# Norm factors, output order and filler steps of the soft-disc layer in a four-layer image kernel

## The chip, the cores and the metric

The kernel runs on one core of a Trainium2 chip. A core has five engines that work at the same time and wait for each other through semaphores: TensorE (PE, matrix products, with weight loads on a path of their own, PEld), VectorE (DVE), ScalarE (ACT), GpSimd (POOL) and SyncE (SP, which here only starts transfers). The metric is the device time of one execution in microseconds (us), as the median of several runs; lower is better.

## The reference

The input is eight images of 32 by 32 tokens with 256 channels in fp32. Four layers follow one another, each of the form x = x + layer(group_norm(x)). Only the last layer is changed:

```python
qkv = silu(x @ w_qkv.T);  q, k, v = split(qkv, 3)
q, k = rope(rms_norm(q, w_qn)), rope(rms_norm(k, w_kn))     # per head of 32
wp = silu(x @ w_wp.T + b_wp);  width_raw, sharp_raw = split(wp, 2)
width = sigmoid(width_raw) * max_dist + 0.5
sharp = sigmoid(sharp_raw) * 9.5 + 0.5
scores = einsum(q, k in a 7x7 window) * 32**-0.5
soft_mask = sigmoid((width - rel_dist) * sharp)
attn = softmax(scores - (1 - soft_mask) * 10000)
out = rms_norm(attn @ v_window, w_on)                        # over 256 channels
return silu((out + v) @ w_out.T)
```

(The rope turns q and k of one head by the same angle at every token, so it falls out of their product and the kernel has no step for it.)

## The kernel before, in words

Channels lie on the 128 partitions, so an image is two chunks of 128 channels (J = 2b + c, four heads each) by 1024 tokens. In `layer3` the attention of a chunk is cut into 8 groups of two 8 by 8 blocks of queries against a window of 14 by 14 keys; with 8 images that makes 128 groups n. A group goes through `DiscStream`:

- `scores(n)`: 8 small products of 32 channels on PE, into four PSUM banks;
- `soft(n)`: four ACT tanh, the disc mask, written into one of nine `e` tiles; `masked(n)`: POOL adds the window's edge;
- `logits(n)`: DVE joins scores and mask and takes the row's extreme;
- `exps(n)`: four ACT exponentials with their sums; `divide(n)`: DVE reciprocal, POOL product;
- `turn(n, 0 and 1)`: eight PE transposes, each four copied by DVE (`pts`); `values(n)`: 12 PE products, copied by DVE into `oT`.

The order on PE, ACT, DVE and POOL is written out by hand: the loop over n at the end of `layer3` emits, in step n, scores(n+3), exps(n), filler units due at n, logits(n+3), turn(n-2, 0), soft(n+5), divide(n), units due at n+0.5, turn(n-2, 1), values(n-3), masked(n+5). All PSUM tiles share one ring of 8 banks. Every engine takes its instructions in the emitted order.

All other work of the layer is a `Fillers` unit with a due step, so that it falls between the groups. For chunk J, n = 8J; for image b, n = 16b:

- `project(J, s, h)` (s = 0 q, 1 k, 2 v; h = half of 512 tokens): two PE products, ACT tanh, DVE product (silu), POOL square for q and k. k and q are due at n-12 to n-10.5, v at n-7.5 and n-7.
- `roots(J, t)`, due at step 8J-8: sums of squares on PE for the two halves of q and k (rows 0 to 127 of one bank) and, for the image two back, of the attention output; then ACT computes exp(-0.5 ln(.)). Ln needs another ACT table than tanh, so two table loads go with it.
- `head_scale(J, s, h)`: spreads one 32-row strip of the factors to 128 partitions by a PE product with K = 32 (`fac_ps`), and DVE multiplies q or k by it. Four units per chunk, due at n-6, n-5.5, n-5, n-4.5.
- `vturn(J, u)`: four PE transposes of the padded v, copied from PSUM by ACT (`v<-vt`). Five units per chunk.
- `tail_sq`, `tail_scale(J, b, c, h)`, `output(b, m, h)`, `reload(b, m, h)`: the end of an image: POOL squares, the norm's factor by a PE product with K = 32 whose weights `won` hold w_on, DVE product, POOL add of v, output projection, silu, residual add, store. tail_scale at n+30 to n+31.5, outputs at n+33.5, 39, 39.5 and 41.5.
- `gn.stats`, `gn.mean`, `gn.root`, `normed`, `discs(b, u)`: the next image's statistics, its normalised copy `xq` (ACT), and the gates of the discs: 16 PE products of 128 columns, then a chain DVE, ACT, DVE, ACT, DVE, DVE, DVE on 128 by 64 values.

A unit may return its second half; `units(at)` collects these in `later`, and `finish()` runs them, two times in a step:

```python
def finish():
    while later:
        later.pop(0)()
```

## Time and profile before

| what | value |
|---|---|
| runs | 3299.59, 3302.94, 3300.57 us; median 3300.57 |
| profiled execution | 3305.0 us, span 3303.2 us, so 1.8 us lie around the span |
| mean granted TensorE clock | 0.973 |
| layer 3, from its first group's exponentials to the end | 2531.9 to 3303.2 us of the span |
| head factors, L2144 | 128 PE instructions (64 products of two passes), 83.9 us busy |
| tail factors, L2177 | 64 PE instructions (32 products), 33.4 us busy |
| copies of the turned v on ACT, L1771 | 80, 573 ns each |
| tanh of the soft mask, L2103 | 512, 543 ns each |
| exponentials, L1715 | 512, 453 ns each |
| ACT table loads in layer 3 (L2136, L2103, L2027) | 18 + 16 + 2, 1283 ns each |

An fp32 product is two PE instructions, one per pass. "Busy" of a line is the union of its instructions' times, so products that run side by side in the array count once. The ends of matmuls are modelled; the distance from one start to the next is the safer figure. The profiled execution lies 4.4 us (0.13%) above the median.

### The profile page before, as it was taken

How to read it: one execution, taken by the hardware profiler on the slowest of the kernel's cores; microseconds unless marked ns; L12 is line 12 of the kernel's file. 1: busy time of each engine (PE TensorE's matmuls, PEld its weight loads, DVE VectorE, ACT ScalarE, POOL GpSimd, SP SyncE). 2: the span in 40 equal slices, each digit the busy share in tenths (PEclk: the TensorE clock that was granted, in tenths of full speed). 3: DMA queues.
4: the chain of work that ended last, by engine and by line, in shares of the span. 5: the costliest groups of instructions: out<-in, count | busy, mean ns of one | idle time of the engine just before them, and what ended most of it. 6: DMA issues, size and time to landing. Idle time of an engine off the chain costs nothing. (4 is left out here: it accounts for less than half of the span.)

```text
span 3303.2 us, 76346 instructions
## 1 busy us (share of the span) xinstructions
PE 3165.7 (96%) x30280; PEld 1638.2 (50%) x30280; DVE 2192.5 (66%) x5570; ACT 2278.5 (69%) x5066; POOL 1792.1 (54%) x1201
## 2 busy tenths in 40 slices
PE   7999999999998999899999999999998899999997
PEld 2323323323322444777777656666664555555554
DVE  4777777777785677565655546666664667777775
ACT  3667667667776567666555547677676878888885
POOL 4666666666663111344444445433436668788777
PEclk9999999999999999999999999999998879999999
DMA  3000000000011667787867630111111001110001
GB/s 142 1 26 10 17 26 1 26 26 1 26 39 57 235 233 260 208 206 204 182 192 205 182 138 28 66 41 40 53 55 44 2 14 40 34 37 30 27 27 62
DMA packets 139177, 267.92 MB, mean 81 GB/s; under 512 B 9218, under 2 KB 77700, under 8 KB 130500
## 3 DMA queue, kind: packets, MB, share of 16 engines
q1 hardware_dynamic: 132436, 242.67, 24.3%
q10 hardware_dynamic: 6384, 20.37, 1.8%
q8 instruction: 239, 3.92, 0.5%
q14 instruction: 118, 0.97, 0.1%
HBM read 177.81 MB, written 85.20 MB: 80 GB/s over the span
## 5 line engine op out<-in xcount | busy, mean ns | idle before, releaser
L694 DVE TENSOR_TENSOR e<-s,ret 128x1024 f32<-128x1024 f32 x512 | 602.1, 1217 | 174.4 <-PE s L688 171.9
L701 ACT ACTIVATE ea<-e 128x1024 f32<-128x1024 f32 x512 | 535.5, 1055 | 257.3 <-DVE e L694 234.9
L703 POOL TENSOR_TENSOR ea<-ea 128x1024 f32<-128x1024 f32 x128 | 304.1, 2376 | 284.9 <-ACT ea L701 216.9
L688 PE MATMUL s<-qk,qk 32*128 32x512 f32 x2048 | 302.1, 640 | 4.3 <-POOL qk L571 1.7
L1591 POOL TENSOR_TENSOR e<-e,su 128x616 f32<-128x616 f32 (+2 forms) x128 | 157.3, 1229 | 268.7 <-DVE su L1590 241.9
L740 PE MATMUL num<-e,v 128*32 128x512 f32 x2048 | 271.3, 595 | 0.0
L1738 DVE COPY pts<-pt 112x512 f32<-112x512 f32 x256 | 175.8, 687 | 137.5 <-PE pt L1733 135.7
L2103 ACT ACTIVATE e<-win,disc 128x196 f32<-128x196 f32 x512 | 239.5, 543 | 0.2
L1723 POOL TENSOR_TENSOR e<-e,su 128x784 f32<-128x784 f32 x128 | 191.4, 1495 | 87.9 <-DVE su L1722 62.0
L870 PE MATMUL up_ps<-x,wup 128*128 128x512 f32 x512 | 230.2, 604 | 4.0 <-POOL x L236 3.2
L1715 ACT ACTIVATE e<-e,mx 128x196 f32<-128x196 f32 x512 | 227.9, 453 | 0.0
L2110 POOL TENSOR_TENSOR e<-e,win 128x784 f32<-128x784 f32 x128 | 201.7, 1576 | 38.5 <-issue 31.6
L1282 POOL TENSOR_TENSOR decayed<-state,rb 128x520 f32<-128x520 f32 x48 | 50.8, 1058 | 304.2 <-PE sc L1215 112.7
L1586 ACT ACTIVATE e<-e,mx 128x154 f32<-128x154 f32 (+2 forms) x512 | 212.2, 425 | 0.0
L1086 ACT ACTIVATE d<-d,cols 128x128 f32<-128x128 f32 x512 | 163.9, 392 | 68.5 <-POOL d L1077 68.4
L713 PE MATMUL sm<-ea,ones 128*32 128x512 f32 x1536 | 208.8, 604 | 1.6 <-POOL ea L703 1.6
L897 DVE SCALAR_TENSOR_TENSOR cv<-xm,par,cv 128x512 f32<-128x512 f32 x192 | 144.7, 754 | 85.8 <-ACT cv L892 81.2
L2042 PE MATMUL qkv_ps<-xq,w 128*128 128x512 f32 x384 | 192.2, 627 | 1.2 <-ACT fac L2137 1.2
L1823 PE MATMUL qkv_ps<-x,w 128*128 128x512 f32 x384 | 182.7, 613 | 1.6 <-POOL x L236 1.6
L688 PEld LDWEIGHTS s<-qk,qk 32*128 32x128 f32 x2048 | 84.8, 182 | 197.2 <-issue 87.7
L1733 PEld LDWEIGHTS pt<-idg,e 128*112 128x112 f32 x1024 | 121.5, 140 | 122.5 <-issue 91.0
L1733 PE MATMUL pt<-idg,e 128*112 128x128 f32 x1024 | 166.5, 289 | 8.4 <-DVE oT L1757 3.1
(245 smaller groups left out, 6932.8 us busy)
## 6 DMA issues: line engine op xcount, KB each, us to landing
d<-l1rows SPq DMA_DIRECT2D x64, 512.0 KB
x<-x SPq DMA_DIRECT2D x25, 1024.0 KB
l1xm<-xm SPq DMA_DIRECT2D x16, 1024.0 KB
l1sz<-sz SPq DMA_DIRECT2D x16, 1024.0 KB
xv<-l1xm SPq DMA_DIRECT2D x32, 512.0 KB
l1xa<-xa SPq DMA_DIRECT2D x16, 1024.0 KB
xa<-l1xa SPq DMA_DIRECT2D x16, 1024.0 KB
rb<-l1rows SPq DMA_DIRECT2D x32, 512.0 KB
```

Source lines behind the costliest of these rows:

```text
L688: nc.tensor.matmul(s[:, j % 2], qk[b, 1, c][g, kb * P : (kb + 1) * P], qk[b, 0, c][g, h * HALF : (h + 1) * HALF], start=True, stop=True,)
L694: nc.vector.tensor_mul(e[n, i], s, m)
L701: nc.scalar.activation(ea[n, i], e[n, i], AF.Abs)
L703: nc.gpsimd.tensor_add(ea[n, i], ea[n, i], ea.pop((n - 1, i)))
L713: nc.tensor.matmul(acc["sm"][g, :], ones, two[j // 2][:, j % 2, :], start=kb == 0 and k == 0, stop=kb == 4 and k == 2,)
L740: nc.tensor.matmul(acc["num"][g, :], v[b][:, kb, vc], e[n, j // 2][:, j % 2, :], start=kb == 0, stop=kb == 7,)
L870: nc.tensor.matmul(ps, wup[:, kc, m * P : (m + 1) * P], seg(s)[:, kc], start=kc == 0, stop=kc == 1,)
L1586: self.nc.scalar.activation(p[:, j], p[:, j], AF.Exp, scale=-1.0, bias=mx[:, j : j + 1], accum_out=su[:, j : j + 1],)
L1715: self.nc.scalar.activation(e[:, j], e[:, j], AF.Exp, scale=-1.0, bias=mx[:, j : j + 1], accum_out=self.su[:, j : j + 1],)
L1733: self.nc.tensor.transpose(ps[: self.PART, at : at + P], self.tile(n)[:, 2 * i + j, k * self.PART : (k + 1) * self.PART], self.K.ident,)
L2103: nc.scalar.activation(e[:, j], win[:, 0], AF.Tanh, scale=disc[b][:, i, 8 + h : 9 + h], bias=disc[b][:, i, h : h + 1],)
L2110: nc.gpsimd.tensor_add(e, e, win[:, 1].unsqueeze(1).to_broadcast([P, 4, NWIN]))
```

## The change

The diff does seven things, all in layer 3 and its preparation. (1) `head_scale(J, s)` issues the products of both halves together, into two banks; there are two units per chunk, due at n-6 (k) and n-5 (q). (2) `tail_scale(J, b, h)` spreads the bare factor with a weight matrix that has ones in row 8 of each strip (`k_one8`), once for both chunks of channels; w_on is now a per-partition operand of the DVE product, which becomes a scalar_tensor_tensor. Two units per image instead of four, at n+27.5 and n+28.5. (3) `output` goes by half first, at n+29.5, 30.5, 31, 31.5, with reloads at n+26.5, 27.5, 28, 30.5. (4) The copy of the turned v goes from ACT to DVE, in the following `finish()`. (5) `discs` is due at n-13 and n-12.5 and its chain is cut into five parts, one per `finish()`; `finish()` keeps what a part returns for the next time. (6) In the steps with n a multiple of 8, `soft(n+5)` is emitted before the units, v's second half before `roots`, and a further `finish()` and `units(n + 0.25)` behind logits; `exps(n+1)` is emitted in step n in place of `exps(n)`. (7) The next image's statistics, its normalised copy and v's projections get other due steps.

```diff
@@ -88,6 +88,7 @@
         [(p[:, None] // 32 == np.arange(32)[None]) / 32.0, one / 256.0], 1
     ).astype(f)
     k["k_spread"] = (p[:, None] % 32 == p[None] // 32).astype(f)
+    k["k_one8"] = np.tile(p[:, None] % 32 == 8, (1, P)).astype(f)
     return {n: np.ascontiguousarray(v) for n, v in k.items()}
 
 
@@ -143,7 +144,7 @@
     a["l3_qkn"] = np.concatenate(
         [np.tile(i["L3_conv_w_" + n], 4) for n in ("qn", "kn")]
     )
-    a["l3_on"] = i["L3_conv_w_on"].reshape(2, P)
+    a["l3_on"] = _cols(i["L3_conv_w_on"])
     a.update(shape_constants())
     return {n: np.ascontiguousarray(v) for n, v in a.items()}
 
@@ -393,13 +394,11 @@
                 spread[:, 0], won[:, 0], -(32.0**-0.5) / MASK_SCALE, spread[:, 0],
                 ALU.mult, ALU.mult,
             )
-            nc.vector.memset(won, 0.0)
 
         def weight():
-            for h in range(2):
-                nc.sync.dma_start(
-                    self.won[32 * h + 8 : 32 * h + 9], a["l3_on"].unsqueeze(0)
-                )
+
+            nc.sync.dma_start(self.won[:, 0], a["k_one8"])
+            nc.sync.dma_start(self.won[:, 1, 0:2], a["l3_on"])
 
         return [loads, factors, weight]
 
@@ -1669,7 +1668,7 @@
 
     def __init__(self, K, wk, cp, pp, pairs, n_img, ebufs):
         super().__init__(K, wk, pp, pairs, n_img, ebufs)
-        self.slots, self.s = 20, {}
+        self.slots, self.s, self.su = 20, {}, {}
         shape = [P, 4, 2 * self.PART]
         self.tiles = [cp.tile(shape, F32, name=f"e{i}") for i in range(ebufs)]
 
@@ -1710,17 +1709,17 @@
 
     def exps(self, n):
         mx, e = self.mx.pop(n), self.prob(n)
-        self.su = self.wk.tile([P, 4], F32, name="su", bufs=4)
+        su = self.su[n] = self.wk.tile([P, 4], F32, name="su", bufs=4)
         for j in range(4):
             self.nc.scalar.activation(
                 e[:, j], e[:, j], AF.Exp, scale=-1.0, bias=mx[:, j : j + 1],
-                accum_out=self.su[:, j : j + 1],
+                accum_out=su[:, j : j + 1],
             )
 
     def divide(self, n):
-        e = self.prob(n)
-        self.nc.vector.reciprocal(self.su, self.su)
-        self.nc.gpsimd.tensor_mul(e, e, self.su.unsqueeze(2).to_broadcast([P, 4, NWIN]))
+        e, su = self.prob(n), self.su.pop(n)
+        self.nc.vector.reciprocal(su, su)
+        self.nc.gpsimd.tensor_mul(e, e, su.unsqueeze(2).to_broadcast([P, 4, NWIN]))
 
     def turn(self, n, i):
 
@@ -1768,7 +1767,7 @@
                 strips[:, col, 8 * r : 8 * r + 8].rearrange("p i j -> p (i j)"),
                 self.K.ident,
             )
-        self.nc.scalar.copy(
+        return lambda: self.nc.vector.tensor_copy(
             dst[: self.PART, 4 * u : 4 * u + 4, :],
             ps[: self.PART, :].rearrange("p (s c) -> p s c", c=P),
         )
@@ -1995,7 +1994,8 @@
         for i in range(3):
             st.clear(i)
         K.ring = st.ring
-        bwp, sel, spread, won = first.bwp, first.sel, first.spread, first.won
+        bwp, sel, spread = first.bwp, first.sel, first.spread
+        ones, on = first.won[:, 0], first.won[:, 1, 0:2]
         wo, win, eps = first.wo, first.win, first.eps
 
         gn = first.gn
@@ -2083,10 +2083,25 @@
                     d, ps.rearrange("p (t g) -> p t g", g=P)[:, :, 0:16],
                     bwp.unsqueeze(1).to_broadcast([P, 4, 16]),
                 )
-                th = wk.tile([P, 4, 16], F32, name="dth")
-                nc.scalar.activation(th, d, AF.Tanh)
+                return silu
+
+            def silu():
+                th = wk.tile([P, 4, 16], F32, name="dth", bufs=2)
+                nc.scalar.activation(th, disc[b][:, 4 * u : 4 * u + 4, :], AF.Tanh)
+                return lambda: silu2(th)
+
+            def silu2(th):
+                d = disc[b][:, 4 * u : 4 * u + 4, :]
                 nc.vector.scalar_tensor_tensor(d, th, 1.0, d, ALU.add, ALU.mult)
+                return sigmoid
+
+            def sigmoid():
+                d = disc[b][:, 4 * u : 4 * u + 4, :]
                 nc.scalar.activation(d, d, AF.Tanh, scale=0.5)
+                return scales
+
+            def scales():
+                d = disc[b][:, 4 * u : 4 * u + 4, :]
                 wd, sp = d[:, :, 0:8], d[:, :, 8:16]
                 md = math.sqrt(2.0) * 3
                 nc.vector.tensor_scalar(wd, wd, md / 2, md / 2 + 0.5, ALU.mult, ALU.add)
@@ -2138,14 +2153,17 @@
             nc.scalar.activation(r[:n], r[:n], AF.Exp, scale=-0.5)
             fac[J] = r
 
-        def head_scale(J, s, h):
-            g = slice(32 * (2 * s + h), 32 * (2 * s + h) + 32)
-            ps = st.ring("fac_ps")
-            nc.tensor.matmul(ps, spread[g, s], fac[J][g], start=True, stop=True)
+        def head_scale(J, s):
+
+            ps = [st.ring("fac_ps") for _ in range(2)]
+            for h in range(2):
+                g = slice(32 * (2 * s + h), 32 * (2 * s + h) + 32)
+                nc.tensor.matmul(ps[h], spread[g, s], fac[J][g], start=True, stop=True)
 
             def rest():
-                d = dest(J, s, h)
-                nc.vector.tensor_mul(d, d, part(ps))
+                for h in range(2):
+                    d = dest(J, s, h)
+                    nc.vector.tensor_mul(d, d, part(ps[h]))
 
             return rest
 
@@ -2164,22 +2182,26 @@
             b, c = divmod(J, 2)
             if u == 0:
                 st.v[b, c] = wk.tile([P, st.slots, P], F32, name="v", bufs=2)
-            st.value_unit(strips, st.v[b, c], u)
+            return st.value_unit(strips, st.v[b, c], u)
 
 
         def tail_sq(b, c):
             sqs["o", c] = wk.tile([P, L], F32, name="sq", bufs=4)
             nc.gpsimd.tensor_mul(sqs["o", c], st.o[b, c], st.o[b, c])
 
-        def tail_scale(J, b, c, h):
+        def tail_scale(J, b, h):
+
             g, hs = slice(32 * h, 32 * h + 32), slice(h * HALF, (h + 1) * HALF)
             ps = st.ring("fac_ps")
-            nc.tensor.matmul(ps, won[g, c], fac[J][g], start=True, stop=True)
+            nc.tensor.matmul(ps, ones[g], fac[J][g], start=True, stop=True)
 
             def rest():
-                d = st.o[b, c][:, hs]
-                nc.vector.tensor_mul(d, d, ps)
-                nc.gpsimd.tensor_add(d, d, vT[b, c][:, hs])
+                for c in range(2):
+                    d = st.o[b, c][:, hs]
+                    nc.vector.scalar_tensor_tensor(
+                        d, d, on[:, c : c + 1], ps, ALU.mult, ALU.mult
+                    )
+                    nc.gpsimd.tensor_add(d, d, vT[b, c][:, hs])
 
             return rest
 
@@ -2217,45 +2239,45 @@
             for i in range(4):
                 s, h = 1 - i // 2, i % 2
                 fill.add(n - 12 + i / 2, lambda s=s, h=h: project(J, s, h))
-                fill.add(n - 6 + i / 2, lambda s=s, h=h: head_scale(J, s, h))
-            fill.add(n - 7.5, lambda: project(J, 2, 0))
-            fill.add(n - 7, lambda: project(J, 2, 1))
+            for s in range(2):
+                fill.add(n - 5 - s, lambda s=s: head_scale(J, s))
+            fill.add(n - 8.5, lambda: project(J, 2, 0))
+            fill.add(n - 8, lambda: project(J, 2, 1))
             fill.add(n - 6, lambda: in_strips(J))
 
         def plan_image(b):
             n = 16 * b
             if b:
                 fill.add(n - 27.5, lambda: load(b))
+                ahead = (n - 23.75, n - 23.75, n - 22.5, n - 21.5)
                 for i in range(4):
                     fill.add(
-                        max(n - 23.5, -3) + i / 2,
+                        ahead[i] if b > 1 else -3 + i / 2,
                         lambda i=i: gn.stats(b, image_parts(x[b]), i),
                     )
                 fill.add(max(n - 21, -1), lambda: gn.mean(b, later))
                 fill.add(max(n - 19, 1), lambda: gn.root(b, later))
                 for c in range(2):
-                    fill.add(n - 13.5 + c / 2, lambda c=c: normed(b, c))
+                    fill.add(max(n - 15, 2) + c / 2, lambda c=c: normed(b, c))
                 for u in range(2):
-                    fill.add(n - 10 + u / 2, lambda u=u: discs(b, u))
+                    fill.add(max(n - 13, 4) + u / 2, lambda u=u: discs(b, u))
             for c in range(2):
                 fill.add(n + 19 + c, lambda c=c: tail_sq(b, c))
-                for h in range(2):
-                    fill.add(
-                        n + 30 + c + h / 2,
-                        lambda c=c, h=h: tail_scale(2 * b + 4, b, c, h),
-                    )
+                fill.add(n + 27.5 + c, lambda c=c: tail_scale(2 * b + 4, b, c))
+
+
             for i in range(4):
-                at = n + 32 + (1.5, 7, 7.5, 9.5)[i]
-                fill.add(at - 3, lambda i=i: reload(b, i // 2, i % 2))
-                fill.add(at, lambda i=i: output(b, i // 2, i % 2))
+                h, m = divmod(i, 2)
+                fill.add(n + (26.5, 27.5, 28, 30.5)[i], lambda h=h, m=m: reload(b, m, h))
+                fill.add(n + (29.5, 30.5, 31, 31.5)[i], lambda h=h, m=m: output(b, m, h))
 
         for J in range(2 * n_img + 3):
             b, c = divmod(J, 2)
             t = b - 2 if c == 0 and b >= 2 else None
+            if J < 2 * n_img:
+                plan_chunk(J)
             if J and (J < 2 * n_img or t is not None):
                 fill.add(8 * J - 8, lambda J=J, t=t: roots(J, t))
-            if J < 2 * n_img:
-                plan_chunk(J)
         for b in range(n_img):
             plan_image(b)
         for J in range(2 * n_img):
@@ -2272,18 +2294,20 @@
                     later.append(r)
 
         def finish():
-            while later:
-                later.pop(0)()
+
+            due = later[:]
+            later[:] = [r for r in [f() for f in due] if callable(r)]
+
+        def all_of(*rests):
+            while rests:
+                rests = [r for r in [f() for f in rests] if callable(r)]
 
         def start():
 
             units(-11)
             rest = [discs(0, 0), discs(0, 1), project(0, 1, 0)]
-            rest[0]()
-            rest[2]()
-            r = project(0, 1, 1)
-            rest[1]()
-            r()
+            all_of(rest[0], rest[2])
+            all_of(rest[1], project(0, 1, 1))
             soft(0)
             for h in range(2):
                 project(0, 0, h)()
@@ -2294,8 +2318,8 @@
             masked(0)
             roots(0, None)
             in_strips(0)
-            for i in range(4):
-                head_scale(0, 1 - i // 2, i % 2)()
+            for s in (1, 0):
+                head_scale(0, s)()
             masked(1)
             for i in range(3, 9):
                 st.clear(i)
@@ -2311,15 +2335,22 @@
                     if t is pairs[0]:
                         st.o[b, c] = wk.tile([P, L], F32, name="oT", bufs=5)
                     st.scores(n + 3)
-                if 0 <= n < N:
-                    st.exps(n)
+                if 0 <= n + 1 < N:
+                    st.exps(n + 1)
+
+                rooted = n % 8 == 0
+                if rooted and 1 < n + 5 < N:
+                    soft(n + 5)
                 units(n)
                 if 0 <= n + 3 < N:
                     st.logits(n + 3)
+                if rooted:
+                    finish()
+                    units(n + 0.25)
                 if 0 <= n - 2 < N:
                     st.turn(n - 2, 0)
                 finish()
-                if 1 < n + 5 < N:
+                if not rooted and 1 < n + 5 < N:
                     soft(n + 5)
                 if 0 <= n < N:
                     st.divide(n)
```

## The prediction

> **What bounds the kernel now.** I read the page first (busy shares, slices, clock), then the table of stretches cut at each image's first exponential in layer 3, then the chain of waits and PE's timeline there. Only layer 3's instructions change their order (before it, layer 2's end alone loses a memset of DVE and swaps two tiny loads), so everything up to 2487 us of the span stays.
>
> ```profile
> span 3303.2 us, 76346 instructions
> PE 3165.7 (96%) x30280; PEld 1638.2 (50%) x30280; DVE 2192.5 (66%) x5570; ACT 2278.5 (69%) x5066; POOL 1792.1 (54%) x1201
> PEclk9999999999999999999999999999998879999999
> ```
>
> The clock dips in slices 31 to 33, the start of layer 3. The stretches (us; busy time and instructions of PE, PEld, DVE, ACT, POOL; granted clock; DMA) are images 0, 1, 2, 3, then 6, 7 and the tail:
>
> ```profile
> 2531.90:2631.40 99.50, 91.72 (x849) 50.54 (x844) 61.43 (x254) 78.85 (x229) 60.95 (x46) 0.80 0.04 12
> 2631.40:2735.40 104.00, 98.32 (x906) 53.17 (x908) 64.52 (x252) 79.28 (x230) 66.02 (x49) 0.80 0.04 12
> 2735.40:2828.00 92.60, 90.08 (x964) 50.40 (x960) 69.44 (x268) 80.88 (x233) 73.97 (x56) 0.98 0.11 36
> 2828.00:2919.20 91.20, 88.69 (x972) 49.63 (x964) 69.36 (x268) 80.99 (x234) 74.06 (x56) 1.00 0.12 36
> ...
> 3101.50:3197.80 96.30, 94.00 (x960) 51.19 (x953) 66.26 (x257) 80.91 (x233) 73.35 (x55) 0.93 0.07 23
> 3197.80:3259.70 61.90, 55.41 (x755) 33.47 (x744) 45.40 (x190) 59.91 (x186) 52.01 (x37) 0.97 0.11 36
> 3259.70:3303.20 43.50, 32.04 (x206) 14.14 (x205) 17.01 (x36) 10.47 (x21) 27.25 (x21) 0.87 0.24 79
> ```
>
> A steady image takes 91.2 us; images 0, 1 and 6, with clock 0.80 and 0.93, take more though they have no more work. Is 88.7 us of busy PE real work? The chain of waits gives start-to-next-start costs (start, us, what):
>
> ```profile
> 2936.30 0.52 PE s L1692 x16
> 2936.83 1.05 PE fac_ps L2144 x2
> 2937.88 0.58 PE pt L1733 x4
> ...
> 2940.09 0.58 PE o L1749 x24
> ...
> 2943.54 1.72 PE qkv_ps L2042 x4
> ```
>
> By these rows and their neighbours (transposes 0.44 or 0.58, projections 1.72 or 1.92, vt 0.44, disc products 1.98, root sums 1.06 and 1.70) an image needs 16 x (0.52 + 0.58 + 2 x 0.51) = 33.9, 16 projections and outputs x 1.82 = 29.1, 12 factor products x 1.05 = 12.6, 10 vt = 4.4, discs 4.0, sums 3.8: 87.8 us. So PE waits only 3.4 us of 91.2 and sets the pace; ACT (80.9), POOL (74.0) and DVE (69.4) follow closely. The waits sit where the chain leaves PE: at the roots on ACT (two table loads of 1.28 us around 0.69 and 0.63, chain pieces from 2918.7 to 2926.9) and at the disc chain from 2955.3 to 2966.9.
>
> The half clock shows in two stretches, same columns:
>
> ```profile
> 2541.00:2558.10 17.10, 17.05 (x97) 7.81 (x98) 10.25 (x43) 14.70 (x44) 11.72 (x10) 0.50 0.20 61
> 2640.00:2663.90 23.90, 23.32 (x157) 11.15 (x158) 13.72 (x59) 15.35 (x48) 15.36 (x11) 0.50 0.14 45
> ```
>
> PE is busy throughout, at half speed. Each such stretch begins two or three steps after a chunk's v projection and ends within a window of the next full 128 by 128 projections (2557.59). In between only factors (32 rows), scores, transposes and values run.
>
> **The change part by part.** (1) *Paired head factors.* Two products in different 32-row strips. The trace has the case: in the start-up, four are adjacent. PE's timeline:
>
> ```profile
> 2512.17 1.14 PE L2144 MATMUL fac_ps<-fac,spread 32*128 32x512 f32 x8 [1.98 <-ACT fac L2138]
> ...
> 2748.60 1.12 PE L2144 MATMUL fac_ps<-fac,spread 32*128 32x512 f32 x2 [0.15 <-ACT v L1771]
> ```
>
> Four together (8 instructions) take what one takes alone, so a pair saves one unit: 1.05 us, about 2.0 at half clock (2542.67 to 2544.67). 15 chunks x 2 = 30 units. DVE's products stay. (2) *One tail factor for both channel chunks*: 2 units of 4 fall away per image, 16 in all. Together 46 x 1.05 = 48 us of PE at full clock, 6.3 per steady image: 87.8 to 81.5. DVE's product keeps form and size (0.68 us).
>
> The Trainium skill ("TensorE: Matmul & The Clock Gate", Part 3) gives 3.07x for four row tiles at N=512, where these rows give 4 x 1.12 / 1.14 = 3.9x. If a pair's loss is taken in proportion, my estimate from that page is 0.8 us saved per pair, 7 us less in all; the measured rows are used.
>
> (3) *v copies, ACT to DVE*: 10 per image x 0.57 = 5.7 off ACT (80.9 to 75.2); on DVE the same shape from PSUM is the pts copy, 0.69 us, so 69.4 + 6.9 = 76.3. Both stay below PE's 81.5, so it costs nothing in the sum; DVE is its cover, and in steps 1, 2, 6 (copies beside head products or vt) it is fuller than PE. If that cover fails PE waits for banks: up to 6.9 per image.
>
> (4) *Roots, soft first, exps one step ahead*: the same two loads per root (18 + 16 + 2 stay). Nothing is removed, but the mask that logits needs two steps later no longer queues behind 3.9 us of loads, Ln and Exp. Behind the root now stand exps(n+2), the second load, and soft of the next step; their users on DVE and PE come two to three steps later. (5) *Disc chain in five parts*: it no longer holds DVE and ACT while each waits for the other. (4) and (5) bear on the 3.4 us of waits: gain 0 to 3.4 per image; I take 0, because DVE and POOL get fuller. Statistics, norms and disc products in other steps: the same instructions and no DMA moved (the next image's load keeps its step); hidden as before under PE's pace, 0; if the norm (2 x 1.13 on ACT) now falls behind a root's loads with no slack, at most 2.3 per image.
>
> (6) *Outputs and reloads*: same four of each. On SP the last reload is one step ahead of its use instead of three; a reload takes about 3 us and a step 5.3, so it is covered; if not, POOL waits, at most 3 us per image, two steps of slack behind it. The three outputs of image 6 that now lie behind the loop move into it (3 x 1.8 of PE, in steps 121 to 127 where PE has idle time). For image 7 the order by half lets output projections start after two of four POOL adds (2 x 1.27 sooner), and no foreign tanh stands before the last root: tail -5, bounds 0 and -8.
>
> **Sum**, against the profiled 3305.0: images 2 to 5: 4 x 5.7 = 23 (6.3 less 0.6 for new waits). Images 0 and 1: four dipped chunks save two units of 2.0 each, 16, less 2 for dips that last longer: 14. Image 6 (one dipped chunk): 8. Image 7, where ACT sets the pace (59.9 of 61.9): 5 vt copies off ACT: 2. Tail 5. Together 52: 3253; the median lies 4.4 below the profiled execution: **3249**. Own range 3235 to 3262.
>
> **The rivals.** *Half gain.* Four engines now lie within 6 us of each other per image, and PSUM's 8 banks let PE lead DVE by about one step only. If DVE and POOL hold PE in the short steps, an image takes 88.5, images 0, 1, 6 gain half: 3274. For: in steps 1 and 2 PE needs 2.6 and 3.2 us by the rows above, while DVE's logits, copies, reciprocal and head products need about 3.3 and 3.9; and POOL meets strips, tail adds and squares in steps 10 to 13. Against: none of the sums passes 76.3.
>
> *Larger gain.* The waits go too (image 82.5, 4 x 8.7 = 35) and the half-clock stretches shorten, since discs now come in step 3 and bring full-array work: images 0 and 1 -13 each, 6 and 7 -14, tail -6: 3305 - 81 - 4.4 = 3219. For: most waits sit just where the order changes.
>
> *Slower: half clock in every chunk.* The change takes the second v projection (step 1) and one output (1.5) out of the stretch after the roots; in odd chunks steps 9, 10 and 11 then hold only small products. The clock falls although PE is busy: in the window 3114.5 to 3117.9 PE is busy 3.24 of 3.40 us and the next ones run at 0.50, with no more than factors, transposes, values and scores in it. A dip lasts 13.6 to 23.9 us and costs up to half, say 8. About six new ones eat the gain; in ten of the eleven chunks now free of a long one: 3249 + 80 = 3329. Against: the steady images have such steps (2 and 3, 10 and 11) already, with one short dip, and if PE is late it runs through them in 6 us.
>
> By the Trainium skill (same page, Part 1) the clock halves after an idle window of about 3.4 us and returns after a busy one. The rows disagree: it stayed at 0.50 for 17.1 us with PE busy for 17.05. By the page's rule a dip would cost some 1.7 us (an estimate) and this rival would never decide.
>
> *The change does nothing*: PE's unit is hidden by something else: 3301. The 3.4 us of waits speak against it.
>
> **How the numbers follow.** Forecast 0.45, half gain 0.25, larger gain 0.18, slower 0.09, nothing 0.03. Range 3208 to 3290: from beyond the larger gain to beyond half gain, leaving out the slower case, the null case and ends. The runs shown spread 3.3 us, so 0.2% (6.6 us) is what can be told from no change. Faster: 0.45 + 0.25 + 0.17 = 0.87; same 0.04; slower 0.09.
>
> **What would show it.** Right: pairs of factors as four instructions in about 1.14 us; the factor products of both lines busy some 60 us in layer 3 instead of 83.9 + 33.4; steady images near 85.5 with ACT 75, DVE 76; table loads still 36. Wrong: low clock in images 2 to 5 in steps 9 to 11; PE waits for pts, v or th in steps 1, 2 and 6; POOL waits for xr. The prediction fails if PE's busy share of a steady image falls below 90%, since then its saved units bought idle time.

## The result and the profile after

| kernel | median | runs | ratio to before | profiled execution | span |
|---|---|---|---|---|---|
| before | 3301.76 us | 3299.59 to 3305.27 (4) | 1 | 3305.0 us | 3303.2 us |
| after | 3253.18 us | 3249.47 to 3256.44 (4) | 0.9854 [0.9838, 0.9869] | 3252.73 us | 3250.8 us |

The time came out 4 us from the forecast of 3249. The terms behind it did not come out so well: two large ones missed, in opposite directions, so the closeness of the total is in part luck, and most of what follows is about that. The same page lines as before, of the changed kernel (span; busy time of each engine; granted clock by slice):

```profile
span 3250.8 us, 76370 instructions
PE 3117.7 (96%) x30248; PEld 1628.4 (50%) x30248; DVE 2244.0 (69%) x5649; ACT 2239.4 (69%) x4986; POOL 1799.2 (55%) x1201
PEclk9999999999998999999999999999999899999998
```

PE is 48.0 us less busy, ACT 39.1 less, DVE 51.5 more: the v copies have moved. The clock's dip where layer 3 begins (8, 8 and 7 in slices 31 to 33) has shrunk to a single 8, in slice 32.

To see where the 52.4 us of span went, layer 3 is cut at the same instructions in every kernel: VectorE's logits of group 3, 11, 19 and so on (line 1704 after), each eight steps later; the last cut is at group 127. Two such stretches are an image, the first called even, the second odd. "Low" is the time at half clock, from the clock records of the same trace. All in us.

| stretch | before | low | after | low | gained | forecast |
|---|---|---|---|---|---|---|
| images 0 and 1 | 205.6 | 81.6 | 173.9 | 17.1 | 31.7 | 14 |
| images 2 to 5 | 366.1 | 3.4 | 364.8 | 34.1 | 1.3 | 23 |
| image 6 | 96.4 | 13.7 | 85.4 | 0 | 11.0 | 8 |
| image 7, to group 127 | 56.3 | 3.4 | 47.1 | 3.7 | 9.2 | 2 |
| the rest | 47.8 | 11.2 | 46.5 | 19.2 | 1.3 | 5 |

(Layer 3 began 2 us later in the changed kernel's execution.) The four images that the forecast called steady gained next to nothing, and the first two twice what was expected. Here are an even and an odd stretch of the kernel before (us; busy time and instructions of PE, PEld, DVE, ACT, POOL; granted clock; DMA):

```profile
2829.30:2876.20 46.90, 44.44 (x492) 26.16 (x488) 34.34 (x135) 41.69 (x119) 37.96 (x29) 1.00 0.13 40
2876.20:2920.40 44.20, 44.15 (x472) 23.41 (x468) 34.91 (x135) 39.20 (x115) 36.00 (x29) 1.00 0.10 33
```

and the like in the changed kernel, an even and an odd stretch of a steady image, then the odd one of image 6:

```profile
2801.20:2841.20 40.00, 38.47 (x477) 24.01 (x476) 35.46 (x136) 37.59 (x112) 35.94 (x26) 1.00 0.15 48
2841.20:2891.20 50.00, 49.48 (x478) 26.40 (x477) 39.97 (x143) 38.59 (x112) 39.16 (x31) 0.93 0.09 28
...
3111.80:3157.20 45.40, 45.23 (x473) 24.37 (x472) 36.24 (x133) 38.35 (x112) 38.31 (x30) 1.00 0.10 33
```

The even stretch fell from 46.9 to 40.0; the odd one rose from 44.2 to 50.0, with a granted clock of 0.93 in place of 1.00. Image 6, with no half clock, took 85.4 (it has no statistics of a next image to compute; these are small on PE).

**What the pairs did.** PE's timeline in the changed kernel (start, us, what, idle before and its releaser): first a pair in image 0, then the two pairs of an odd stretch and what comes after them.

```profile
2538.48 1.13 PE L2161 MATMUL fac_ps<-fac,spread 32*128 32x512 f32 x4
...
2849.38 1.93 PE L2161 MATMUL fac_ps<-fac,spread 32*128 32x512 f32 x4
2851.24 1.08 PE L1732 MATMUL pt<-idg,e 128*112 128x128 f32 x8
2852.25 0.65 PE L1748 MATMUL o<-pts,v 112*32 112x128 f32 x24
2852.83 0.59 PE L1691 MATMUL s<-kp,qT 32*64 32x196 f32 x16
2853.37 1.72 PE L2161 MATMUL fac_ps<-fac,spread 32*128 32x512 f32 x4
```

The pair of image 0 takes what the prediction gave it, 1.13 us for four instructions. The other two take 1.93 and 1.72. From the start of the second to PE's next product pass 2.06 us, nearly as much as two single factors; 0.34 us of that PE is idle, because the next product (line 201) waits for a copy on DVE. The weight loads of that second pair (same columns) and VectorE's products with the pair before it tell why:

```profile
2853.37 0.29 PEld L2161 LDWEIGHTS fac_ps<-fac,spread 32*128 32x128 f32 x2 [0.30 <-DVE kp L2166]
2853.96 0.29 PEld L2161 LDWEIGHTS fac_ps<-fac,spread 32*128 32x128 f32 x2 [0.30 <-DVE kp L2166]
```

```profile
2852.64 1.27 DVE L2166 TENSOR_TENSOR kp<-kp,fac_ps 128x512 f32<-128x512 f32 x2
```

DVE multiplies by the first pair only at 2852.64, over three us after its first product, and is done at 2853.9. The second half of the next pair waits until DVE has finished (2853.91 against a weight load at 2853.96), so it starts 0.59 us after the first half instead of beside it. What PE needs from DVE there can only be a free PSUM bank; the factors were ready long before. Over the whole run this is the largest share of these weight loads' waits, 8.8 us (29 times):

```profile
L2161 PEld LDWEIGHTS fac_ps<-fac,spread 32*128 32x128 f32 x128 | 17.4, 182 | 20.3 <-DVE kp L2166 8.8 <-issue 3.9 <-DVE pts L1737 3.9
```

(the last columns: idle time of the weight queue before these loads, and what ended it). The four pairs of a steady image take 1.36, 1.65, 1.86 and 2.06 us from start to next start, 6.9 together, where eight singles took 8.4.

**What the clock did.** Three windows right after the second pair, same columns as the stretches above:

```profile
2852.40:2855.80 3.40, 3.06 (x47) 1.50 (x41) 3.37 (x10) 3.40 (x12) 3.34 (x4) 1.00 0.01 2
2855.80:2862.60 6.80, 6.80 (x52) 3.46 (x52) 6.20 (x24) 4.16 (x16) 4.54 (x5) 0.50 0.01 4
2862.60:2866.00 3.40, 3.40 (x12) 1.52 (x10) 2.10 (x10) 1.83 (x5) 2.78 (x3) 1.00 0.00 0
```

In the first window PE is busy 3.06 of 3.40 us, but with scores, factors of 32 rows and transposes. The next 6.8 us are granted half clock (0.50), though PE is busy throughout. The clock is back after the first projection of 128 by 128 (2861.71). The prediction's slower rival described this. In images 2 to 5 it happens in steps 11 to 13 of the odd stretches, 3.4 or 6.8 us each time, 23.9 us in all. The other 10.2 of the 34.1 us lie in even stretches and begin otherwise, behind waits of PE for DVE's qT (line 2052) of 1.86 and 2.61 us.

### The profile page after: what moved, and what is told of

The parts are those of the page before. It is cut to its first block, busy times and chain, and to the rows that moved or that the text cites. A ratio compares the mean times of both kernels' runs of the same rounds, so it can differ in the third digit from the quotient of the medians.

```text
span 3250.8 us, 76370 instructions
## 1 busy us (share of the span) xinstructions
PE 3117.7 (96%) x30248; PEld 1628.4 (50%) x30248; DVE 2244.0 (69%) x5649; ACT 2239.4 (69%) x4986; POOL 1799.2 (55%) x1201
## 5 line engine op out<-in xcount | busy, mean ns | idle before, releaser
L1704 DVE CUSTOM_DVE_ANT_0 e<-s,e 128x196 f32<-128x196 f32 x512 | 153.5, 354 | 12.8 <-POOL e L2125 11.3
L1732 PE MATMUL pt<-idg,e 128*112 128x128 f32 x1024 | 157.3, 284 | 4.8 <-POOL e L1722 2.2
```

## Experiments

All are timed with the kernel before beside them on the same chip, whose medians there were 3301.9, 3303.0, 3307.1 and 3307.2 us; so ratios are compared. The question behind them is whether the forecast's mechanism (PE units saved) holds and half clock takes part of it, or whether another part of the change (order, copies, discs, outputs) earned the time; a theory's letter counts for its run alone. The columns "even" and "odd" are the averages of images 2 to 5; all columns from "images 0, 1" on are of the profiled execution.

| kernel | median us | ratio [95%] | images 0, 1 | images 2 to 5 | low there | even | odd |
|---|---|---|---|---|---|---|---|
| before | 3301.8 | 1 | 205.6 | 366.1 | 3.4 | 46.9 | 44.6 |
| after | 3253.2 | 0.9854 [0.9838, 0.9869] | 173.9 | 364.8 | 34.1 | 41.6 | 49.6 |
| u1_single | 3260.3 | 0.9876 [0.9852, 0.9900] | 183.9 | 357.9 | 6.8 | 42.1 | 47.4 |
| h1_pairs_late | 3265.9 | 0.9892 [0.9865, 0.9919] | 181.7 | 369.2 | 37.5 | 42.3 | 50.0 |
| h2_v_mid | 3310.6 | 1.0025 [1.0013, 1.0037] | 187.9 | 395.7 | 54.6 | 51.1 | 47.8 |
| u6_order | 3321.6 | 1.0059 [1.0040, 1.0079] | 190.6 | 399.0 | 68.3 | 46.9 | 52.9 |
| h5_dummy | 3249.9 | 0.9841 [0.9824, 0.9859] | 177.4 | 359.2 | 10.2 | 41.3 | 48.5 |
| h4_disc_split | 3240.4 | 0.9811 [0.9797, 0.9826] | 170.7 | 355.0 | 3.4 | 39.4 | 49.3 |
| u5_disc_back | 3260.4 | 0.9870 [0.9855, 0.9884] | 177.1 | 368.4 | 30.7 | 40.6 | 51.5 |
| u4_v_act | 3269.0 | 0.9894 [0.9877, 0.9910] | 175.0 | 374.1 | 44.4 | 44.0 | 49.5 |
| h6_split_late | 3241.0 | 0.9809 [0.9782, 0.9836] | 169.7 | 355.7 | 13.7 | 39.8 | 49.1 |
| h7_split_single | 3237.7 | 0.9803 [0.9769, 0.9837] | 170.5 | 347.2 | 0 | 38.4 | 48.4 |
| b6_order | 3302.9 | 0.9999 [0.9980, 1.0018] | 198.8 | 377.8 | 30.7 | 48.6 | 45.8 |
| u3_outs_back | 3281.2 | 0.9937 [0.9914, 0.9960] | 170.0 | 379.9 | 41.0 | 51.8 | 43.2 |

**The pairing undone.** Four single factors per chunk, at their old dues (`head_scale` and the start-up, not shown, go back with the plan):

```
-            for s in range(2):
-                fill.add(n - 5 - s, lambda s=s: head_scale(J, s))
+            for i in range(4):
+                s, h = 1 - i // 2, i % 2
+                fill.add(n - 6 + i / 2, lambda s=s, h=h: head_scale(J, s, h))
```

> The change with the pairing of the head factors undone: four single units per chunk at n-6 to n-4.5, the rest as changed. A single unit takes 1.05 us from start to next start; the changed kernel's 30 pairs took 1.06 to 2.21, some 1.67 each. Theory A (pairs are half hidden: the second product waits for a PSUM bank): 30 x (2.10 - 1.67) = 13 us more, 3266. Theory B (the pairing is worth the full unit, as forecast): 31 to 40 us more, 3284 to 3293. Theory C (PE does not set the pace, the units are hidden): 3253.

7 us slower than the change, by medians; the intervals overlap. The parts point both ways: images 0 and 1 lost 10 us, with 20 more at half clock, and images 2 to 5 gained 7 although PE had more factors to do, since their half clock shrank from 34.1 to 6.8.

**The pairs half a step later**, after the products that hold their banks (`n - 5 - s` becomes `n - 4.5 - s`):

> The changed kernel with both pairs half a step later (n-5.5 and n-4.5), behind logits, the first transposes and a finish of the same step, when DVE has emptied four score banks. Theory A (the second product of a pair waits for DVE to free a bank): the four instructions start together, a pair takes about 1.07 us, some 18 us of PE time less; 3240 if PE sets the pace. Rival (two products alone do not run side by side in the array unless four are adjacent): pairs stay at 1.4 to 2.1 us and the time at 3253.

A miss in the time. The pairs did become cheaper (1.38, 1.06, 1.56 and 0.96 to 2.01 us from start to next start, 42.1 over the layer in place of 51.5), and the kernel no faster: 13 us slower by medians, though the intervals touch, with 8 us lost in images 0 and 1 and 4 in images 2 to 5, half clock in every odd stretch (6.8 us) and more often in the even ones.

**One full-width product more in odd stretches**, two accumulating 128 by 128 matmuls into a bank nobody reads (the unit `warm` itself is not shown):

```
+            if b:
+                fill.add(16 * b - 5, lambda b=b: warm(b))
```

> The changed kernel plus one full 128 x 128 product (K 256, 512 columns, 1.72 us on PE at full clock) at step 11 of every odd chunk but the last, into a bank that nothing reads: pure extra work. Theory D (the odd chunks of 49.4 us are long because a window with only small products halves the clock at step 11 or 12): low clock there vanishes, odd chunks 44.8 + 1.7 = 46.5, five dipped chunks gain 2.9 each, the undipped one loses 1.7: 3253 - 13 = 3240. Rival (low clock is a by-product of a wait): seven times 1.7 is added, 3265.

The odd stretches' half clock vanished, and 1.8 us of added work per image made the kernel no slower: 3249.9. The direction is shown; the size (3 us, not told apart from nothing by the intervals) is less than expected. The odd stretch fell only from 50.0 to 48.5.

**The second disc unit in that place instead**, work that must be done anyway:

```
-                    fill.add(max(n - 13, 4) + u / 2, lambda u=u: discs(b, u))
+                    fill.add((max(n - 13, 4), n - 5)[u], lambda u=u: discs(b, u))
```

> The changed kernel with the second disc unit (16 products of 128 columns at full array, 1.98 us) moved from step 3.5 of the even chunk to step 11 (n-5) of the odd chunk; nothing added. Theory D: low clock at steps 11 to 13 vanishes, odd chunks 44.8 + 2.0 = 46.8, even chunks 40.6 - 1.5 = 39 if one disc unit is enough for their clock: an image 86 instead of 90 to 92, five of them: 3253 - 23 = 3230. Rival (the even chunks then lose their own full-array work and dip): even 43 to 45, 3250.

3240.4 us: faster than before and than the change (the intervals do not overlap), though 10 us short of what was expected. Half clock in images 2 to 5 is back to 3.4 us. An image without any still takes 88.7 us (same columns as the stretches above):

```profile
2884.60:2923.90 39.30, 37.18 (x461) 22.40 (x460) 35.10 (x131) 37.30 (x110) 34.64 (x26) 1.00 0.17 49
2923.90:2973.30 49.40, 48.85 (x494) 26.89 (x493) 42.55 (x149) 39.03 (x114) 39.25 (x31) 1.00 0.09 29
```

PE is busy 86.0 of it, and half clock explains nothing here. So the pairs' price had to be tested without it, in the two runs told last.

**The v projection and the strips later**, to spread full-width work over the odd stretches:

```
-            fill.add(n - 8, lambda: project(J, 2, 1))
-            fill.add(n - 6, lambda: in_strips(J))
+            fill.add(n - 5.5, lambda: project(J, 2, 1))
+            fill.add(n - 4.5, lambda: in_strips(J))
```

> The changed kernel with the second half of v's projection moved from step 0 (n-8) to the middle of step 2 (n-5.5) of each chunk, and the strips from n-6 to n-4.5. Nothing is added. Theory D (in odd chunks the clock is halved because steps 9 to 12 hold only small products): full 128 x 128 work there keeps the clock at 1.00 in images 1 to 5, odd chunks fall from 49.4 to about 45 us, 3253 - 20 = 3233. Rival (the low clock only follows a wait and costs nothing itself): odd chunks stay near 49 us, 3253. Rival (later strips and v hold up the transposes of v): slower, 3260.

Slower than the kernel before. It kept the odd stretches at 47.8, and opened a wait of 7.9 us in the even ones. PE's timeline (idle time and releaser in brackets) and ScalarE's there:

```profile
2929.92 1.13 PE L2161 MATMUL fac_ps<-fac,spread 32*128 32x512 f32 x4
2938.98 3.51 PE L2075 MATMUL wp_ps<-w,xq 128*128 128x128 f32 x16 [7.93 <-DVE vT L2054]
```

```profile
2929.74 1.28 ACT L2118 ACT_TABLE_LOAD   x1
2931.03 1.88 ACT L2118 ACTIVATE e<-win,disc 128x196 f32<-128x196 f32 x4
2932.82 1.23 ACT L418 ACTIVATE xq<-x,gn 128x1024 f32<-128x1024 f32 x1
...
2935.71 1.86 ACT L2118 ACTIVATE e<-win,disc 128x196 f32<-128x196 f32 x4
2937.47 0.57 ACT L2027 ACTIVATE th<-qkv_ps 128x512 f32<-128x512 f32 x1
```

The tanh of the v projection (line 2027) stands on ACT behind a table load, two soft discs, a norm and four exponentials; DVE's product for vT waits for it, and a bank with it, and PE for the bank. After it the disc products run at half clock (3.51 us for 16; the next 16 take 1.95).

**The order inside a step undone** (exponentials, soft and finish where they were; nothing else):

> The changed kernel with the loop's order as before: exps(n) in step n, soft(n+5) behind the first finish in every step, no extra finish in root steps; the rest as changed. Theory E (the new order takes the waits at the roots off the chain): even chunks go from 40.6 back to 43 or 44 us, 16 x 2 to 3 us, 3285 to 3300. Rival (the order is worth nothing, the gain is PE's work and the outputs' place): 3253.

3321.6, slower than the kernel before: worse than both theories expected. In this kernel the order is worth 68 us. PE's longest waits in layer 3 say where part of it goes (us, times, longest):

```profile
PE fac_ps L2161 <- DVE pts L1737: 20.2, 14, 2.3
```

The second half of a pair now stands some 2 us for a bank, and half clock comes with it: such a wait of 2.06 us ends at 2830.15, and from 2830.3 on the clock is at half for 10.2 us. **The same order alone in the kernel before**:

> The kernel before with one part of the change only: the order inside a step (row exponents one step ahead, soft and finish moved round the roots). Undoing this order in the changed kernel cost 68 us, with 68 us at half clock in images 2 to 5. Theory N (the order matters there because the changed kernel has less PE work to cover waits behind ACT; the kernel before has 3.4 us at half clock in images 2 to 5 and gaps of only 2.5 us per image): gain of 0 to 25 us, 3278 to 3302, most of it in images 0 and 1 (205.6 us, of it 82 at half clock). Rival O (the order is worth the same anywhere): 3235 us, faster than the whole change.

Nothing: 0.9999 [0.9980, 1.0018]. Images 0 and 1 gained 6.8, image 6 gained 6.0 and images 2 to 5 lost 11.7. So the order is no gain that adds to the others. The kernel before has single factors, so the wait that the order spares the pairs of the changed kernel does not exist there; that this is the whole reason was not tried.

**The v copies back on ACT**:

```
-        return lambda: self.nc.vector.tensor_copy(
+        self.nc.scalar.copy(
```

> The changed kernel with the copy of the turned v back on ACT, at once behind its transposes. By the sums ACT would need 80.9 and DVE 69.4 of the 85 to 90 us of an image, so by the forecast's working the edit is worth nothing: 3253. Rival (ACT is late behind the roots' loads, the copy of step 1.5 queues there and holds its bank): one stall of 2 to 4 us per chunk, 3253 + 16 x 3 = 3300.

16 us slower by medians, where the prediction's sum had nothing: the copies' move earned time, in images 2 to 5 (9 us), image 6 (5) and the end (6). Half clock in images 2 to 5 rose by 10 us. The wait that the rival named is there:

```profile
PE s L1691 <- ACT v L1770: 13.9, 7, 2.2
```

Six of these seven waits last 2.20 us, and in five of the six cases half clock begins within 1.3 us of the wait's end, before or after it.

**The discs and norms back** to their old dues:

> The changed kernel with the disc units and the normalised copy at their steps of before (n-10, n-9.5; n-13.5, n-13), the chain still cut into five. Theory F (images 0 and 1 gained 32 us because the discs in step 3 or 4 bring full-array work early and keep or restore the clock): low clock returns in even chunks, 6 to 13 us each, even chunks 40.6 to 45, 3253 + 8 x 4 = 3285. Rival (the gain there is the loop's order alone): 3253.

7 us slower by medians, not 32, and the intervals overlap. Images 0 and 1 kept nearly all that they had gained; their half clock came back to 30.7 us, from 17.1, where the kernel before has 81.6. So the early discs freed them of a small part of it at most.

**Outputs, reloads and tail factors back** to their old dues (their order by halves kept):

```
-                fill.add(n + 27.5 + c, lambda c=c: tail_scale(2 * b + 4, b, c))
+                fill.add(n + 30 + c, lambda c=c: tail_scale(2 * b + 4, b, c))
...
-                fill.add(n + (29.5, 30.5, 31, 31.5)[i], lambda h=h, m=m: output(b, m, h))
+                fill.add(n + (33.5, 39, 39.5, 41.5)[i], lambda h=h, m=m: output(b, m, h))
```

> The changed kernel with the tail factors, reloads and output units at the dues of the kernel before (2.5 to 10 steps later; the order of their halves as in the changed kernel). In the trace the sixteen output products that took 7.05 us of PE in image 7 before are in images 0 and 1 in the changed kernel, and image 7 went from 56.3 to 47.1 us. Theory P (that move is what image 7 gained, and only moves work about): image 7 back to 54 to 56, images 0 and 1 shorter by 5 to 7 or the same if PE waits there instead, the tail 48; 3253 to 3262 us. Rival Q (the units also give PE full-width work that keeps the clock up in images 0 and 1): images 0 and 1 go from 174 back to 190 us with 20 us or more at half clock, 3275 us or more.

28 us slower, and neither theory foresaw where: image 7 went to 53.6, the end to 49.5 and images 0 and 1 to 170.0, near P, but images 2 to 5 lost 15 and image 6 lost 7. PE's waits over layer 3 (us, times, longest) and the timeline show it:

```profile
PE fac_ps L2161 <- DVE th L2219: 13.6, 11, 2.3
```

```profile
2803.10 1.12 PE L2161 MATMUL fac_ps<-fac,spread 32*128 32x512 f32 x2
2806.54 1.12 PE L2161 MATMUL fac_ps<-fac,spread 32*128 32x512 f32 x2 [2.32 <-DVE th L2219]
```

An output product runs one step ahead of the pair (2799.31); its bank is free only when DVE has done the output's last product (line 2219). The second half of the pair needs a bank and stands 2.3 us. This is the pairs' weakness again, with another holder. Five of these waits last 2.32 us, and half clock begins within 2 us of the end of each, before or after it.

**Pairs cheap and the clock up, both at once**: the second disc unit at `n - 5` and the pairs half a step later.

> The changed kernel with two moves together: the second disc unit at due n - 5 instead of n - 12.5 (step 11 of each odd chunk, as in h4_disc_split, which took 3240.4 us), and the paired head factors half a step later (as in h1_pairs_late, where a steady image's pairs take 42.1 / 8 = 5.3 us of PE against 6.9 in h4_disc_split, but half clock came to steps 11 to 13). Theory K (two separate deductions from the forecast: pairs that wait for a PSUM bank, and half clock in odd chunks; each move mends one): 88.6 - 1.6 = 87.0 us per image in images 2 to 5, no half clock there, 3240 - 7 * 1.6 = 3229 us. Rival L (later pairs take PE's cover out of steps 11 to 13 again, disc unit or not): half clock of 6.8 us in odd chunks, 3250 us or more.

The pairs took 39.6 us over the layer in place of 51.6 in h4_disc_split, a 12 us saving of PE, and the time did not move (3241.0 against 3240.4). K fell; L too, since the 13.7 us of half clock in images 2 to 5 all lie in the even stretches. **Split discs with single factors**:

> The second disc unit at due n - 5 and the pairing undone (four single head factors per chunk at their old dues): what the pairing is worth once half clock is out of the comparison. Theory K: in h4_disc_split the eight pairs of an image take 6.9 us of PE and the sixteen single factors of the kernel before 8.4, so singles cost 1.5 us per image, 12 in all: 3252 us (the prediction's step 1 would say 4.2 per image and 3274). Rival M: single factors free their banks in turn, so the waits of the logits and turns near the pairs vanish too and nothing is lost: 3240 us or less.

3237.7, no slower than with pairs: h6_split_late, beside it on the same chip, has 3241.0, and the intervals overlap. M holds: a loss of a few us would not show in these intervals, but the 34 us of the prediction's step 1 would. (An image has four pairs, or eight singles; the "eight" and "sixteen" of the expectation are twice that, its us are right.) Of all kernels tried this has the lowest median, and its ratio and those of the two others with split discs lie below the change's. Where PE's time in layer 3 goes, summed from each product's start to the next start (waits and half clock included; totals of the profiled executions, of which h7's, 3231.9 us, lies 5.8 below its median):

| product | before | after | h4_disc_split | h6_split_late | h7_split_single |
|---|---|---|---|---|---|
| head factors | 78.6 | 50.5 | 50.6 | 37.8 | 61.3 |
| tail factors | 34.8 | 22.4 | 18.5 | 18.8 | 18.4 |
| scores s | 85.4 | 87.6 | 102.1 | 99.6 | 83.9 |
| turns pt | 162.3 | 148.9 | 133.2 | 141.1 | 135.9 |
| disc products | 25.7 | 25.6 | 26.3 | 33.3 | 26.3 |

(The head factors of the start-up, 1.0 to 1.8 us, are left out.) What pairs save in their own row comes back elsewhere: from h7 to h4 the factors fall by 10.7 and the scores rise by 18.2; from h4 to h6 factors fall by 12.8 while turns and discs rise by 15. In h7 single factors even found partners without being told, a head and a tail factor from other strips next to each other in PE's queue (starts 2843.60 and 2843.61, both 0.69):

```profile
2843.60 0.69 PE L2159 MATMUL fac_ps<-fac,spread 32*128 32x512 f32 x1
2843.61 0.69 PE L2193 MATMUL fac_ps<-fac,won 32*128 32x512 f32 x1
2844.13 0.59 PE L2159 MATMUL fac_ps<-fac,spread 32*128 32x512 f32 x1
2844.14 0.59 PE L2193 MATMUL fac_ps<-fac,won 32*128 32x512 f32 x1
```

**Half clock and images 0 and 1.** Over all fourteen kernels the time of images 0 and 1 follows their time at half clock: from 205.6 us with 81.6 low to 169.7 with 6.8, and the straight line through the fourteen points has a slope of 0.50 us per us (single kernels lie up to 6 us off it, u3_outs_back 10). By that line the change's 64.6 us less at half clock there are worth 32 us, all of the 31.7 gained. (The Trainium skill, "TensorE: Matmul & The Clock Gate", Terms, puts the penalty at the throttled time times the share of pulses withheld, which is one half here; these runs agree.)

How half clock begins can be counted. All clock records of a trace lie on one grid of 3.41 us. In images 0 to 6 of the fourteen kernels, 129 stretches of half clock begin. Before 76 of them PE was busy 2.14 us or less in the 3.41 us ahead, around a wait of 1.27 us or more; before the other 53 it was busy 2.46 to 3.41 us, with no product of 128 by 128 (projection, disc product or output). Of the windows at full clock with PE busy 2.2 us or more, none of the 1657 that held such a product was followed by half clock, but 53 of the 601 without one were. The kernel before shows both kinds, each with its window ahead (same columns as the stretches above):

```profile
2588.80:2592.20 3.40, 0.88 (x8) 0.84 (x8) 1.74 (x6) 3.40 (x13) 1.57 (x1) 1.00 0.00 0
2592.20:2612.70 20.50, 20.28 (x150) 9.71 (x149) 14.66 (x61) 11.52 (x38) 10.72 (x8) 0.50 0.00 1
...
2800.40:2803.80 3.40, 3.38 (x27) 1.33 (x16) 3.40 (x15) 3.40 (x13) 3.34 (x4) 1.00 0.27 83
2803.90:2807.30 3.40, 3.40 (x45) 2.17 (x46) 3.21 (x14) 1.11 (x6) 2.96 (x3) 0.50 0.00 0
```

In images 0 and 1, 64.9 of the 81.6 us before belong to the first kind, behind waits of 1.58 to 2.77 us; after the change 6.8 of 17.1 do.

## Why the prediction was right in total, and where it was not

**Step (1), a pair costs one unit of 1.05 us: this failed.** In a steady image the four pairs took 6.9 us, not 4.2; the first pair behind the loop's start (2538.48), whose second half has no wait before it, took 1.06 us from start to next start. The row taken from the start-up came from such a place too: all four products began together there. The half-gain rival had the mechanism, "PSUM's 8 banks let PE lead DVE by about one step only"; without half clock an image takes 88.7 in h4_disc_split, and the rival said 88.5. Beyond its price, the pairing's worth was mistaken: in h7_split_single, where half clock is nearly out of the comparison (0 and 3.4 us in images 2 to 5), undoing it costs nothing measurable. In the changed kernel as it stands, its part in images 0 and 1 (10 us, by u1_single) comes from the clock.

**Step (2), two tail factors fewer per image: right in PE's time.** 4.21 us per image before, 2.10 in images without half clock on them; what it brought in total time is not shown, since no run tried it alone.

**Step (3), v copies at no cost: right that DVE covers them, too low in what they bring.** ACT has 76.2 us in a steady image (75.2 said), DVE 75.4 (76.3 said), and u4_v_act says some 16 us for the move. ACT's relief counts though ACT was not the pace: with the copies on ACT, PE's scores wait 13.9 us until ACT has done such copies, and there is 10 us more half clock in images 2 to 5.

**Steps (4) and (5), waits 0 to 3.4 per image, 0 taken: near the mark in the steady images, but with the wrong picture.** Idle time of PE is 2.0 us in the steady image of the changed kernel against 2.5 before. But the order is not neutral: the changed kernel without it is 68 us slower, while the kernel before gains nothing by it. And the sum priced a wait at its own length, where many of these waits are followed by half clock. The cut of the disc chain into parts was not tried by itself.

**Moves at 0.** Discs and norms: 7 us by medians, with overlapping intervals. Outputs and reloads: 28 us by u3_outs_back, against 0 in the steady images and 5 at the end. The prediction looked at SP's reload (hardly anything waits for it, 0.4 us in all: POOL's xr additions wait for DVE's th, line 2219, 17.1 us) and not at the PSUM bank that an output holds (13.6 us of PE's waits in u3_outs_back). It also overlooked that the four outputs leaving image 7 were 7.05 us of PE, most of the 9.2 gained there; images 0 and 1 took in as many.

**Half clock.** The slower rival's place was right (odd chunks, nearly its steps), its price was too high: the stretches are 3.4 to 6.8 us long and cost about half of that, since a projection in step 13 ends them; 30.7 us more in images 2 to 5 at one half are 15 us. The prediction judged the clock by how long it stays low with PE busy; its own windows show how it falls: PE was busy 0.88 of 3.40 us ahead of 2592.2 and 1.21 ahead of 2640.0, with waits. The larger gain's half-clock stretches in images 0 and 1 did shorten, mostly because these waits went; its reason, discs in step 3, fell with u5_disc_back. Of the single parts undone, the order (17 us) and the pairing (10) cost most there, but the order alone in the kernel before brought 7: waits of 2.75, 2.74 and 2.74 us remain ahead of half clock in b6_order, and without the order others stand there (4.04, 1.66, 1.50 and 2.00 in u6_order). Which combination of parts removes the waits stays open.

**The sum.** Images 2 to 5 fell short by 22 us, for which half clock (some 15) and the pairs (4 x 2.7 = 11) are more than enough; images 0 and 1 gained 18 more than said, image 6 3 more, image 7 7 more, the end 4 less. Even PE's busy time fell by 48.0 us, the prediction's number, with half clock and waits of its own in it. The total came out right because the clock, taken to stay nearly as it was, gave at the start what it and the pairs took in the middle: errors of 22 and 4 us one way and 18, 3 and 7 the other. That they cancel is luck. Of the promised signs, the factor products came to 51.2 + 20.8 = 72.0 us busy, not 60; steady images to 88.5 to 94, not 85.5; the table loads stayed 36; PE was busy 88.0 of 90.0 us, so the sign of failure (below 90%) never showed. That sign could not see this error: a pair in series keeps PE busy too.

## What to carry to other kernels

Before pricing two matmuls as one because they use different rows, look at when both of their PSUM banks come free; the price comes from the busiest place, not from the start-up. Price a wait of PE not at its length alone: look whether half clock follows it. Where the clock also follows the kind of work, as here, a unit of full-width work has a worth of place: spread it so that few windows of 3.4 us are without it, and count a saving as real only in stretches with equal clock. If parts of a change act through shared banks and the clock, undo them one by one *and* try them alone: here one part was worth 68 us in company and nothing alone.

## What the runs showed of the hardware

- Half clock began in two ways: behind a wait of PE of 1.27 us or more (76 of 129 times), and with PE busy 2.46 to 3.41 us of the 3.41 ahead on small products alone (53 times; 3.06 of 3.40 in the window shown first). It then stayed with PE fully busy (6.80 of 6.80 us at 0.50). The Trainium skill ("TensorE: Matmul & The Clock Gate", Part 1) ties the fall to an idle window and the return to a busy one; the 76 fit that in kind, the 53 and the stay do not.
- A product of 128 by 128 that nobody needs (1.8 us) removed the second kind from the odd stretches at no cost in time (3249.9 us against 3253.2).
- Two products in different 32-row strips ran together where they stood next to each other in PE's queue with no wait before the second, also from unrelated lines (starts 0.01 us apart). With the second bank late a pair took 1.72 or 1.93 us instead of 1.13.
